# Issuing one kind of input copy from GpSimd's queue instead of SyncE's, in a polynomial convolution with attention

## The chip, the cores and the metric

The kernel runs on one core of a Trainium2 chip. The metric is the device time of one execution in microseconds. The core has a matrix engine (TensorE, PE in the profile), three engines for elementwise work (VectorE or DVE, ScalarE or ACT, GpSimd or POOL), and SyncE (SP), which in this kernel only issues data transfers (DMAs). Each engine works through its own list of instructions in order and waits at an instruction until the semaphores that it names have been raised.

## The reference

Input `x` has 32 images of 64 channels by 56 x 56 pixels. Layer 0 acts on groups of 8 channels; layer 1 is an attention over the 3136 pixels of each image.

```
# layer 0: second and third order products of the 8 channels of a group
p2 = x[:, :, _I2] * x[:, :, _J2]
y2 = einsum('bgihw,goi->bgohw', p2, W2) + b2
p3 = x[:, :, _I3] * x[:, :, _J3] * x[:, :, _K3]
y3 = einsum('bgihw,goi->bgohw', p3, W3) + b3
y  = x + y2 * beta2 + y3 * beta3 * 0.1
# layer 1, l = y
g     = clip(bn(conv1x1(l, w_inside)), 0, 6)
theta = l[:, :32]
f     = einsum('niab,nicd->nabcd', theta, theta)
f     = softmax(softmax(f, over the first pixel index), over the second)
out   = einsum('nabcd,nicd->niab', f, g) / h * w
out   = bn(depthwise_conv3x3(out, w_dw)) + l
```

## The kernel before, in words

The images are worked on in 16 pairs. For each pair a **stage** of 49 tiles runs (24 tiles of 128 pixel rows for the first image, one tile of both images' last 64 rows, 24 for the second image). A tile's scores come from PE into PSUM in two halves, DVE moves them to SBUF and keeps the minimum (the softmax's shift), ACT makes both exponentials over 128 x 3136 elements, and PE multiplies the result with `g` into the accumulators `av` and `ax`. While the tiles of one pair run, the polynomials (layer 0) of the next pair are worked out in between; the convolution taps of the pair before run on DVE, and the rest is `g`, transposes and stores.

Before the first stage the first image's polynomial is computed by itself (to about 90 us). The first stage then has more to do than the others: the second image of the first pair (chunks called two-image chunks here: 32-row halves `TWO = (2, 3)`) and the whole second pair (four-image chunks, `ALL`; the four are the two images' halves of 32 channels). Later stages work out one pair's polynomials each, 13 four-image chunks.

**A chunk.** The 3136 pixels are cut into 13 chunks of 242 (the last 232). The inputs of a chunk are copies of `x` from HBM whose rows are rotated within the groups of channels, so that a product of two tiles multiplies different channels. Per half there are: `x0`, `xa` (the names of their tiles are x and xa in the profile), `x2`, `x4` (both x in the profile), one copy each, and `xb`, two copies of half the rows. Per chunk there is one tile `xc`, filled by two copies: the channels unrotated and rotated by four. These two are the last that a chunk needs. So SP issues 14 copies for a two-image chunk and 26 for a four-image chunk. POOL multiplies: first `q = x0 * xa` per half, then `p = q * x0`, `q * x2`, `q * x4`, `q * xb` per half, and last one product of the two parts of `xc` (called p4 in the code, p<-xc_None in the profile). These go to PE, which accumulates them in six rounds (`poly`, L455); DVE then adds bias and the unrotated part of `xc` and writes `y` (`poly_out`, L472).

**What sets the order.** A class `Pinned` (its `call`, L107; all its instructions have line L108 in the profile) chains every instruction of an engine to the one recorded before it, so that each engine's list is in the order in which the code was run. The copies stand in `plan`, a list in the order of use. `prefetch` (L357) takes the next copies from it while two conditions hold: a buffer is to be had (`XB`, L318: 7 for `x0`, 13 for `xs`, which is all other rotated tiles, 3 for `xc`), and `credit` is at least 1. Each transfer that `start` (L325) issues costs one credit. `pace` (L943) gives 8 (first stage) or 4.5 (later) credits in each half tile, never more than 8 in hand. `prefetch` is called by `advance` (L413) twice per tile and after each product inside `products` (L365), which releases a buffer. Products are limited by `ROOM` (L362): 8 buffers for `q`, 20 for `p`; a chunk of four has 17 p. Loads of `th` (the theta rows, from `y`), the placing of the transposed attention output in `tt`, and the stores to the output go through `start` too, on SP's queue.

Of the kernel before, what the change touches and what calls it, by code (L numbers as in the profile page):

```python
# [69 lines left out]
def tile_poly_conv_attention(  # L70
# [43 lines left out]
    pe, dve, act, pool, sync = map(Pinned, (nc.tensor, nc.vector, nc.scalar, nc.gpsimd, nc.sync))  # L114
# [17 lines left out]
    at = 0  # L132
    for s, (_, bs) in enumerate(STEPS):
        for h in range(2) if s < NSLOT else ():
            act.dma_start(
                out=wq[s::NSLOT, :, h, :],
                in_=wpoly[h * 32 : h * 32 + 32, at : at + NRND, h * 32 : h * 32 + 32],
# [18 lines left out]
    for k in range(2):  # L156
        pe.matmul(
            out=ax[:, k * 256 : k * 256 + 256],
            lhsT=w4,
            rhs=wq.rearrange("p k h o -> p (k h o)")[:, :256],  # L160
            start=(k == 0),
# [105 lines left out]
    for k in range(NRND):  # L267
        by = row("beta2_0") if k == 0 else b3row
        w = wq[:, k, :, :].rearrange("p h o -> p (h o)")
        dve.tensor_tensor(w, w, by, ALU.mult)  # L270
    for half in (0, C):
        w = w4[:, half : half + C]
# [49 lines left out]
    PACE = 4.5  # L322
    credit = [1e9]

    def start(out, in_):  # L325
        credit[0] -= 1
        sync.dma_start(out=out, in_=in_)

    def load_next():
        tag, key = plan.pop(0)  # L330
        n, c, ks, name, k = key
        p0, w = PCS[c]
        held[tag] += 1
        ident = f"{n}_{c}_{ks[0]}_{k}"
        if name == "c":
            t = xp.tile([128, 2, PCH], FP, name=f"xc_{ident}", tag=tag, bufs=XB[tag])
            at = slice(ks[0] * 32, ks[-1] * 32 + 32)
            for d in range(2):
                src = bass.AP(
                    x.tensor,  # L340
                    ((4 * n + ks[0]) * EXT + 4 * d) * 4 * N + p0,
                    [[EXT * 4 * N, len(ks)], [N, 32], [1, w]],
                )
                start(t[at, d, :w], src)
            loaded[key] = [t[at, d, :w] for d in range(2)]
            return
        t = xp.tile([128, PCH], FP, name=f"x{name}_{ident}", tag=tag, bufs=XB[tag])
        for s0, every, d, grow in LOADS[name]:
            src = bass.AP(
                x.tensor,  # L350
                ((4 * n + k) * EXT + d) * 4 * N + p0,
                [[N, 32], [grow * 4 * N, NSLOT // every], [1, w]],
            )
            start(t[s0::every, :w] if every > 1 else t[:, :w], src)
        loaded[key] = t[:, :w]

    def prefetch():  # L357
        while plan and held[plan[0][0]] < XB[plan[0][0]] and credit[0] >= 1:
            load_next()
# [126 lines left out]
    def load_theta(b, c0=0, c1=N):  # L486
        y = ys[b // 2 % 3]
        p0 = (b % 2) * C
        if c0 == 0:
            ths[b] = thp.tile([128, N], FP, name=f"th_{b}", tag=f"th{b % 2}")  # L490
        for r in range(4):
            start(ths[b][r * 32 : r * 32 + 32, c0:c1], y[p0 : p0 + CRED, c0:c1])
# [365 lines left out]
    for n in range(NP):  # L858
# [8 lines left out]
        if n == 0:  # L867
# [10 lines left out]
            at = [2 * base + free[i * (len(free) - 1) // (len(todo) - 1)] for i in range(len(todo))]  # L878
        elif n + 1 == NP:
            todo = gb  # L880
            at = [2 * (base + LAG) + 3 + 4 * i for i in range(len(gb))]
        else:
            at = []
# [30 lines left out]
        for b, end in ((2 * n, base + NQ), (2 * n + 1, base + IT - 1)):  # L914
            t = end + LAG
# [7 lines left out]
    for n in range(NP):  # L923
# [11 lines left out]
        for i in range(9 * NB):  # L935
            at = more[i * (len(more) - 1) // (9 * NB - 1)]
# [11 lines left out]
    t = 0  # L948
# [117 lines left out]
```

## Time and profile before

| | |
|---|---|
| median of 3 runs | 4949.45 us (4947.52 to 4963.6) |
| the profiled execution | 4948.12 us |
| its span | 4946.3 us, mean granted clock 0.992 |
| PE busy | 4734.2 us (96%) |
| ACT busy | 4554.4 us (92%) |
| DVE busy | 4125.5 us (83%) |
| POOL busy | 3222.6 us (65%) |
| SP's transfers of xc | 416, issue 523 to 751 ns, median 561 |
| DMA, mean | 139 GB/s |

Groups in the profile are named by what they write and read: `p<-q,x` is a product of q and an x tile, `ax<-p,wq` a matmul of the polynomial, `ps<-th` the scores, `av<-gq,e` the attention product. SPq is SP's queue with the time that it takes to issue one transfer; issuing is not counted as an engine's busy time. A wait is told as "who <- whom: us in total, times, longest". In an order of time, a line holds the start, the time taken, the engine and the group, how many instructions are merged in it, and in square brackets how long the engine had been idle and what ended that.

### The profile page before, as it was taken

The numbers are of one execution on the slowest core, as the hardware profiler recorded it, in microseconds if no ns is written. First come the engines' busy times: TensorE is split into PE (matmuls) and PEld (weight loads), VectorE is DVE, ScalarE is ACT, GpSimd is POOL, SyncE is SP. The second block draws the span as 40 slices with busy tenths as digits, with TensorE's granted clock in tenths as the row PEclk, the third lists the DMA queues.
The fourth block names the chain that finished last, engine by engine and source line by source line (L and its number), as shares of the span: only waits on it lengthen the run. The fifth ranks groups of instructions, "written<-read, shape, count | busy, mean of one in ns | idle before, by whom it ended". The sixth has DMA issues, their size and how long they took to land.

```text
span 4946.3 us, 264020 instructions
## 1 busy us (share of the span) xinstructions
PE 4734.2 (96%) x118122; PEld 3218.8 (65%) x118122; DVE 4125.5 (83%) x6100; ACT 4554.4 (92%) x2356; POOL 3222.6 (65%) x4335
## 2 busy tenths in 40 slices
PE   6898999999999999999999999999999999999887
PEld 2555666666666666666666666666666666666665
DVE  6545898888888898888889889898888889888887
ACT  1667999999999999999999999999999999999996
POOL 2677685858858586785857768585875858678000
PEclk8999999999999999999999999999999999999999
DMA  7555656565565655556555565656556565654201
GB/s 205 145 152 156 147 144 153 144 152 141 145 141 151 146 145 149 143 143 146 149 143 144 149 143 142 154 144 150 142 145 143 150 144 144 153 142 126 45 11 34
DMA packets 884318, 685.66 MB, mean 139 GB/s; under 512 B 290924, under 2 KB 869356, under 8 KB 879084
## 3 DMA queue, kind: packets, MB, share of 16 engines
q1 hardware_dynamic: 875180, 659.46, 52.5%
q8 instruction: 924, 15.14, 1.3%
q10 hardware_dynamic: 8000, 9.30, 0.6%
q14 instruction: 214, 1.75, 0.1%
HBM read 565.65 MB, written 25.69 MB: 120 GB/s over the span
## 4 chain that ended last, share of the span: by engine, by line
PE 77%; DVE 12%; DMA 3%; issue 3%; ACT 3%; POOL 1%; SPq 1%; ACTq 0%; DVEq 0%; POOLq 0%
PE av L108 33%; PE ps L108 26%; PE ax L108 18%; DVE e L108 10%; ACT e L108 3%; DMA xc_None<-in_x_dram 1%; POOL p L108 1%; DVE y L108 1%; DMA first<-in_x_dram 1%; DVE num L108 1%; DMA x<-in_x_dram 1%; SPq L108 1%; DMA xa<-in_x_dram 0%; DVE rd L108 0%; ACTq L108 0%
## 5 line engine op out<-in xcount | busy, mean ns | idle before, releaser
L108 PEld LDWEIGHTS av<-gq,e 128*64 128x64 f32 x64512 | 2012.2, 138 | 943.9 <-issue 936.2
L108 ACT ACTIVATE e<-e,nm 128x3136 f32<-128x3136 f32 x784 | 2283.6, 2913 | 279.9 <-DVE e L108 264.0
L108 POOL TENSOR_TENSOR p<-q,x 128x242 f32<-128x242 f32 (+1 forms) x2418 | 1824.3, 788 | 815.6 <-PE ax L108 801.2
L108 ACT ACTIVATE e<-e,rz 128x3136 f32<-128x3136 f32 x784 | 2270.3, 2896 | 0.0
L108 PE MATMUL av<-gq,e 128*64 128x65 f32 x64512 | 2225.5, 225 | 3.9 <-ACT e L108 3.1
L108 DVE TENSOR_SCALAR_CACHE_REDUCE e<-ps 128x1568 f32<-128x1568 f32 x784 | 1403.7, 1790 | 314.1 <-PE ps L108 294.2
L108 DVE TENSOR_SCALAR_CACHE_REDUCE e<-ps,nm 128x1568 f32<-128x1568 f32 x784 | 1448.6, 1848 | 255.7 <-PE ps L108 250.1
L108 PE MATMUL ps<-th 32*64 32x392 f32 x25088 | 1449.4, 515 | 120.7 <-DVE e L108 110.7
L108 POOL TENSOR_TENSOR q<-x,xa 128x242 f32<-128x242 f32 x806 | 574.2, 734 | 226.0 <-DMA xa<-in_x_dram 218.0
L108 DVE SCALAR_TENSOR_TENSOR y<-tt,wdt,y 128x605 f32<-128x605 f32 (+6 forms) x711 | 713.1, 1003 | 6.4 <-DMA tt<-tr 5.2
L108 POOL TENSOR_TENSOR p<-q,xb 128x242 f32<-128x242 f32 x806 | 573.9, 739 | 212.3 <-PE ax L108 204.5
L108 PEld LDWEIGHTS ps<-th 32*64 32x64 f32 x25088 | 369.8, 130 | 463.7 <-DVE e L108 381.5
L108 PE MATMUL ax<-gq,e 128*64 128x65 f32 x12288 | 489.7, 222 | 0.7 <-issue 0.6
L108 PE MATMUL ax<-p,wq 128*32 128x242 f32 (+1 forms) x6448 | 481.9, 374 | 1.8 <-POOL p L108 0.2
L108 PEld LDWEIGHTS ax<-gq,e 128*64 128x64 f32 x12288 | 425.0, 138 | 1.0 <-issue 1.0
L108 PEld LDWEIGHTS ax<-p,wq 128*32 128x32 f32 x6448 | 178.4, 109 | 111.8 <-POOL p L108 19.1
L108 POOL TENSOR_SCALAR y<-y,bias 128x616 f32<-128x616 f32 (+2 forms) x79 | 146.9, 1860 | 98.9 <-PE ax L108 98.9
L108 POOL TENSOR_TENSOR p<-xc_None 128x242 f32<-128x242 f32 (+3 forms) x208 | 127.6, 614 | 109.5 <-DMA xc_None<-in_x_dram 91.0
L108 DVE SCALAR_TENSOR_TENSOR y<-ax,bias,xc_None 128x242 f32<-128x242 f32 (+3 forms) x208 | 97.1, 467 | 116.8 <-PE ax L108 116.8
L108 PE MATMUL ax<-wit,y 128*64 128x64 f32 x3136 | 144.2, 223 | 11.7 <-issue 7.5
L108 PE MATMUL ax<-p,w 128*32 128x242 f32 (+1 forms) x1612 | 123.9, 370 | 32.1 <-POOL p L108 32.1
L108 ACT ACTIVATION_READ_ACCUMULATOR e<-e,nm 128x1 f32 x784 | 145.5, 186 | 0.0
(86 smaller groups left out, 1389.4 us busy)
## 6 DMA issues: line engine op xcount, KB each, us to landing
x<-in_x_dram SPq DMA_DIRECT2D x2232, 121.0 KB
xa<-in_x_dram SPq DMA_DIRECT2D x744, 121.0 KB
xb<-in_x_dram SPq DMA_DIRECT2D x1488, 60.5 KB
th<-y SPq DMA_DIRECT2D x124, 392.0 KB
xc_None<-in_x_dram SPq DMA_DIRECT2D x360, 121.0 KB
x<-in_x_dram SPq DMA_DIRECT2D x186, 116.0 KB
out_dram<-y SPq DMA_DIRECT2D x60, 308.0 KB
tt<-tr SPq DMA_DIRECT2D x128, 100.0 KB
```

Of the source, the lines that this page charges most:

```text
L108: i = f(*args, **kw)
```

## The change

`start` gets an argument for the queue, and the two copies that fill `xc` are given POOL's. POOL's queue is in the same order as its products, so the transfers take a place between these. They no longer cost a credit. The rest of the copies stay on SP's queue. The first pair's first image does not use this code.

```diff
-    def start(out, in_):
-        credit[0] -= 1
-        sync.dma_start(out=out, in_=in_)
+    def start(out, in_, queue=sync):
+        if queue is sync:
+            credit[0] -= 1
+        queue.dma_start(out=out, in_=in_)
...
-                start(t[at, d, :w], src)
+                start(t[at, d, :w], src, pool)
```

In the built program POOL's list then has 416 transfers more, and SP's 416 fewer.

## The prediction

> **What bounds the kernel now.** I went from the widest view to the narrowest: busy time by stretch, who waits for whom, then the queues that the change touches, in order of time. Busy time first: the two parts of the first stage (first pair's missing polynomials, 97 to 213 us, then the second pair's, 213 to 482) beside a later stage. Columns are engine busy times, granted clock, DMA share and GB/s.
>
> ```profile
> core 0: us, PE busy (x) PEld busy (x) DVE busy (x) ACT busy (x) POOL busy (x), PEclk, DMA share, GB/s
> 97.00:213.00 116.00, 100.78 (x1876) 57.25 (x1876) 59.33 (x93) 77.67 (x41) 87.25 (x133) 0.98 0.54 143
> 213.00:482.00 269.00, 243.81 (x5360) 153.56 (x5360) 152.11 (x241) 191.83 (x100) 196.18 (x295) 0.96 0.57 151
> 1615.00:1919.00 304.00, 298.27 (x7652) 205.57 (x7646) 266.27 (x388) 294.60 (x154) 215.08 (x288) 1.00 0.57 144
> ```
>
> In a later stage TensorE (PE) and ScalarE (ACT) are full, 298 and 295 of 304 us, and GpSimd (POOL) has 89 us free. In the first stage nothing is full: ACT does 270 us of work in 385. Something feeds it too slowly. The waits of weight loads (PEld) and matmuls between 97 and 482 say what:
>
> ```profile
> PEld ax L108 <- POOL p L108: 62.3, 63, 3.8
> PE ax L108 <- POOL p L108: 32.3, 20, 3.4
> ```
>
> PE waits 95 us for POOL's products; from 1007 to 4650 it waits for POOL not once. And POOL, over that later stretch:
>
> ```profile
> POOL p L108 <- PE ax L108: 890.4, 291, 28.4
> POOL p L108 <- DMA xc_None<-in_x_dram: 20.0, 14, 2.6
> ```
>
> There POOL is ahead: it waits for PE to free product buffers, 890/3643 of the time, or 74 us in each 304. In the first stage it waits for data instead. The order of time of one four-image chunk, on POOL and on SyncE's queue (SPq):
>
> ```profile
> 430.87 7.98 POOL L108 TENSOR_TENSOR p<-q,x 128x242 f32<-128x242 f32 x12
> 438.79 2.70 POOL L108 TENSOR_TENSOR p<-q,xb 128x242 f32<-128x242 f32 x4
> 444.52 0.62 POOL L108 TENSOR_TENSOR p<-xc_None 128x242 f32<-128x242 f32 x1 [3.03 <-DMA xc_None<-in_x_dram]
> ```
> ```profile
> 428.16 5.63 SPq L108 DMA_DIRECT2D x<-in_x_dram  x8
> 433.88 5.05 SPq L108 DMA_DIRECT2D xb<-in_x_dram  x8
> 439.02 1.17 SPq L108 DMA_DIRECT2D xc_None<-in_x_dram  x2
> 440.24 0.56 SPq L108 DMA_DIRECT2D x<-in_x_dram  x1
> ```
>
> SPq issues without a pause, some 0.65 us from one copy to the next, while DMA engines are 57% busy. The pair xc comes last of its chunk, and POOL stands 3.03 us waiting for it. So the first stage is bound by **SPq's issuing**, with POOL just behind; everything later is bound by PE and ACT.
>
> **What the change does, step by step.** The profiled execution took 4948.1 us (span 4946.3); the median of the runs is 4949.45, 1.3 above. My sums start from 4948.1.
>
> *SPq loses* two of 14 copies in a two-image chunk, two of 26 in a four-image one. By the lines above a pair takes 440.24 - 439.02 = 1.2 us. Two-image chunks: their xc products start at 97.50 and, twelve chunks on, at 213.00, so 9.63 us each; SPq would need 8.4. Four-image chunks: from 259.67 to 481.48 is twelve of 18.5 us (the one before, 28.2 us, holds a 9.35 us wait for PE and is left out); SPq would need 17.3. The copies no longer take credit, but SP's queue keeps its order apart from two things: the first image's th copy of each later pair stands behind two more loads (1.3 us), four tt copies behind two. No PE wait for th was seen from 1007 on, so I cost that at nothing; without cover it is 1.3 us in 14 stages, 18 us.
>
> *POOL gains* 416 copies, and its order shows where: a pair stands between products, 12 to 17 products ahead of the one that needs it (0, 2 and 6 for the first three). Twelve products of 0.665 us are 8.0 us; from the issue of the pair above to its product are 444.52 - 439.02 = 5.5 us. So the 55 us in which POOL waits for xc in this stage go, the first wait apart. Most pairs add a wait for DVE, for the chunk three back to have left its xc buffer. Behind it stand POOL's next products, and for those PE; but these wait in any case for PE to free product buffers of a later chunk (20 buffers, 17 to a chunk), so I cost the wait at nothing; uncovered it is at most DVE's 1.85 us operation ahead of it, in the stage's 26 chunks 48 us.
>
> *What one copy costs POOL's queue* no row shows: nothing was issued there. From below: the same copy on SPq, 0.56 us (median of 416). From above: 2.0 us, POOL's longest regular operation (y<-y,bias, 672 columns, 1.99). I take **1.0 us**, nearest to SPq's row, which is the same work, plus some 0.4 for handing it to the engine's cores (POOL's small operations on 128 partitions, a 128-column memset and a 128-column scaling, take 0.2 and 0.64).
>
> The Trainium skill ("DMA: Bandwidth & Descriptors", Latency and other measured facts) gives about 0.6 us to the first byte from SyncE's queue and about 1 us from GpSimd's; as an estimate by that ratio a copy would cost 0.93 us, and the sum would be 2 us lower than mine.
>
> *The sum.* POOL's own pace, waits taken out: two-image chunk 164.24 - 155.73 - 1.16 = 7.35 us; four-image chunk 444.52 - 427.10 - 3.03 - 0.50 = 13.9. With 2.0 us more: 9.35 and 15.9. Each chunk takes the slower of the two queues.
> - Two-image: max(8.4, 9.35) against 9.63, -0.28 x 12 = -3 us. Relief of one queue is eaten by the other.
> - Four-image: max(17.3, 15.9) against 18.5, -1.2 x 13 = -16 us.
> - Later stages: 26 x 1.0 = 26 us more POOL work in each 304, under 74 us of waiting for PE: 0.
>
> Check on the whole: POOL is busy 283 us of the 385; with 52 it is 335 of 366, 92%, full but not over. All of the gain reaches the end, as PE alone could do such a stage in 304. **4948 - 19 = 4929 us.** At the lower bound, 0.56: two-image max(8.4, 8.47), -14, and -16: 4918. At 2.0: +1.72 x 12 = +21, four-image 17.9, -8: 4961.
>
> One page speaks against the move. DVE's only copies here go to PSUM (ax<-bias1r, 288 of 361 ns) and its large reductions come from PSUM; POOL's products in the first stage run at an even 0.665 us beside them. The skill ("SBUF — State Buffer", SBUF: two separate sides, and the section after it) says that a DVE copy in a two-port mode locks GpSimd out of writing descriptors, and that a copy of about 0.62 us then took about 3.1; as an estimate, by 3.1 the same formula would give 4948 + 48 + 21 = 5017, and by 0.62 about 4920. The trace of before can't show it; as the page asks for both ends in SBUF, I do not take it.
>
> **The rivals.**
> 1. *POOL becomes the bound* (slower). Place: the first stage. Mechanism: POOL is held for the whole of each pair, from issue until its data can be used, 5.5 us by the chunk above, so 2.75 a copy. Two-image chunks 12.85, +3.2 x 12 = +39; four-image 19.4, +0.9 x 13 = +12; later 13 x 5.5 = 72 us just under the 74. 4948 + 51 = **4999**. It passes +0.3% from about 2.05 us a copy. For it: POOL is 73 to 75% busy in the first stage, the tightest place for it. Against: its products do not wait for the copy at once.
> 2. *The relief and the load cancel* (no change). At 1.5 us a copy: two-image 10.35, +9; four-image still SPq's 17.3, -16; sum **4941**. Slots freed later by POOL, behind a pair, would make SPq wait in its turn (it already waits 54 us for p between 90 and 450) and take part of the 16.
> 3. *The copies were not what POOL lacked.* Between 90 and 450 POOL also waits 15 for xa, 18 for PE; if these grow by what xc loses, the 55 us come back and POOL's additions show whole: 52 us at most, less SPq's 31: **4969**.
>
> **Chances.** A change under 0.3%, about 15 us, is no more than this measurement can tell from none. By the formula that means faster below about 1.15 us a copy, slower above about 2.05. Forecast (below 1.15): 0.38. Cancelling (1.15 to 2.05, the shift small): 0.32. Rival 1: 0.20; rival 3: 0.10, both slower. As gains and losses share the chance, the likeliest case's own range is 4918 to 4934. The range reaches from just below the lower bound, 4914, to rival 1's 4999.
>
> **What would show it.** In the changed trace: POOLq with 416 xc issues, their duration the disputed size; POOL's wait for xc between 97 and 482 from 55 to under 6 us; xc products 9.4 us apart in the two-image part, 17.3 in the four-image part; the second part's end (481.5, the first xc product of the third pair) near 463; PE still without a wait for POOL from 1007 on, stages still 304 us. The forecast is wrong if issues are over 1.15 us, if SPq's waits for POOL grow by more than it saves, or if a later stage lengthens: a single us there is 14 in all.

## The result, and the profile after

The changed kernel takes 5317.08 us (median of 4 runs, 5299.51 to 5331.99), the kernel before in the same comparison 4949.88 us. The ratio is 1.073, with a 95% interval from 1.071 to 1.076: 7% slower. The forecast of 4929 us and its range, up to 4999 us, are both wrong.

The profiled execution of the changed kernel took 5331.99 us (span 5330.2). Where do the 384 us over the profiled 4948.12 lie? I count a stage from the read-out that ends ScalarE's (ACT's) first exponential of a pair; these moments, counted from the span's start, split the difference:

| | before | after | difference |
|---|---|---|---|
| second stage begins | 505.9 | 489.1 | -17 |
| mean of the 14 stages that follow, to the start of the last | 293.6 | 322.1 | +28.5 each, +399 |
| from there to the end of the trace | 329.7 | 331.4 | +2 |

So the first stage did about what was forecast, and the later stages lost 28.5 us each on the mean (17 to 36). The later stage of 304 us in the prediction was a window a little longer than a stage, which is 293.6 us.

**The first stage.** Four-image chunk, order of time (start, time taken, engine, group, count, idle before):

```profile
408.92 6.16 SPq L108 DMA_DIRECT2D x<-in_x_dram  x8
...
411.61 1.37 POOL L108 DMA_DIRECT2D xc_None<-in_x_dram  x2
...
412.99 7.94 POOL L108 TENSOR_TENSOR p<-q,x 128x242 f32<-128x242 f32 x12
...
415.18 5.04 SPq L108 DMA_DIRECT2D xb<-in_x_dram  x8
...
420.27 0.59 SPq L108 DMA_DIRECT2D x<-in_x_dram  x1
...
420.90 2.68 POOL L108 TENSOR_TENSOR p<-q,xb 128x242 f32<-128x242 f32 x4
...
423.55 0.61 POOL L108 TENSOR_TENSOR p<-xc_None 128x242 f32<-128x242 f32 x1
```

The pair stands between GpSimd's (POOL's) products, 1.37 us for two copies. SyncE's queue (SPq) goes from xb to the next chunk's x with no xc between them, and the product of xc starts without an idle time in brackets: 3.03 us of waiting are gone.

**The later stages.** The same windows as before (the first two cut at 203 and 459 us, near the new ends of the two parts, 206.4 and 458.5); the third is the later stretch from 1615 to 1919:

```profile
core 0: us, PE busy (x) PEld busy (x) DVE busy (x) ACT busy (x) POOL busy (x), PEclk, DMA share, GB/s
97.00:203.00 106.00, 101.89 (x1806) 55.75 (x1808) 57.30 (x89) 72.65 (x38) 99.84 (x151) 0.97 0.63 160
203.00:459.00 256.00, 243.96 (x5418) 151.60 (x5420) 153.74 (x246) 196.46 (x102) 217.43 (x329) 0.99 0.62 156
1615.00:1919.00 304.00, 280.96 (x7016) 193.06 (x7024) 258.83 (x359) 272.51 (x141) 207.11 (x285) 0.97 0.54 132
```

In the third row ACT is down from 294.60 to 272.51 us and TensorE (PE) from 298.27 to 280.96. Neither is full any more, POOL is not full either, and less data is moved (144 to 132 GB/s). So something makes all of them wait. The waits of the whole run (who waits for whom: us in total, times, longest), first before, then after:

```profile
POOL p L108 <- PE ax L108: 1018.8, 331, 28.4
...
PEld ps L108 <- DVE e L108: 381.5, 886, 3.2
ACT e L108 <- DVE e L108: 264.0, 359, 23.9
...
PE ps L108 <- DVE e L108: 110.7, 256, 2.0
...
POOL p L108 <- DMA xc_None<-in_x_dram: 91.0, 44, 4.9
```
```profile
POOL p L108 <- PE ax L108: 1339.5, 302, 34.4
...
PEld ps L108 <- DVE e L108: 655.6, 896, 9.0
ACT e L108 <- DVE e L108: 651.7, 461, 23.9
PE ps L108 <- DVE e L108: 388.7, 334, 8.5
...
POOL p L108 <- DMA xc_None<-in_x_dram: 7.4, 2, 4.8
```

ACT's wait for VectorE's (DVE's) minimum and move `e` went from 264.0 to 651.7 us, PE's from 110.7 to 388.7. POOL still waits for PE, by 1339.5 us where it was 1018.8: POOL is not the bound, and everything is late behind DVE. What in DVE became longer is told by its groups by shape, before (xcount, busy us, mean ns of one, idle before):

```profile
L108 DVE TENSOR_SCALAR_CACHE_REDUCE e<-ps 128x1568 f32<-128x1568 f32 x784 | 1403.7, 1790 | 314.1 <-PE ps L108 294.2
L108 DVE SCALAR_TENSOR_TENSOR y<-tt,wdt,y 128x605 f32<-128x605 f32 x360 | 370.7, 1030 | 0.0
L108 DVE SCALAR_TENSOR_TENSOR y<-tt,wdt,y 128x616 f32<-128x616 f32 x180 | 167.0, 928 | 0.0
```

and after:

```profile
L108 DVE TENSOR_SCALAR_CACHE_REDUCE e<-ps 128x1568 f32<-128x1568 f32 x784 | 1403.3, 1790 | 362.9 <-PE ps L108 347.4
L108 DVE SCALAR_TENSOR_TENSOR y<-tt,wdt,y 128x605 f32<-128x605 f32 x360 | 556.0, 1544 | 0.0
L108 DVE SCALAR_TENSOR_TENSOR y<-tt,wdt,y 128x616 f32<-128x616 f32 x180 | 249.1, 1384 | 0.0
```

The large reductions take what they took; the convolution **taps** `y<-tt,wdt,y` take half as long again. A mean hides how: of all 711 taps the longest took 1.5 us before; after, 89 took over 2.5 us (I call these held taps), the longest 9.8 us, and the sum went from 713 to 1011 us. One of them in order of time:

```profile
1883.94 2.71 POOL L108 TENSOR_TENSOR q<-x,xa 128x242 f32<-128x242 f32 x4
...
1886.57 1.37 POOL L108 DMA_DIRECT2D xc_None<-in_x_dram  x2
...
1887.95 5.24 POOL L108 TENSOR_TENSOR p<-q,x 128x242 f32<-128x242 f32 x7
...
1888.66 3.97 DVE L108 SCALAR_TENSOR_TENSOR y<-tt,wdt,y 128x616 f32<-128x616 f32 x1
...
1892.55 1.84 DVE L108 TENSOR_SCALAR_CACHE_REDUCE e<-ps,nm 128x1568 f32<-128x1568 f32 x1
...
1894.44 2.91 ACT L108 ACTIVATE e<-e,nm 128x3136 f32<-128x3136 f32 x1 [2.73 <-DVE e L108]
...
1894.46 1.24 PE L108 MATMUL ps<-th 32*64 32x392 f32 x16 [2.60 <-DVE e L108]
```

POOL issues a pair, then runs seven products without a pause. The tap that begins 0.7 us behind the pair takes 3.97 us instead of about 0.9, and ends within the seventh product, which takes 1.23 us where the others take 0.7: only ahead of that one did it get in. The reduction queued behind it on DVE is late, and ACT and PE stand idle for 2.73 and 2.60 us. In all, 73 of the 96 taps that began within 2.5 us behind a pair, without a pause of POOL over 0.15 us between, were held; of other DVE work that began within 1.3 us behind a pair, none grew (49 large reductions and 28 transposes among it).

Not every held tap begins near a pair, but going back from each of the 89 over POOL's list without a pause leads to one. In 14 of them, one in each later stage, POOL's own `y<-y,bias` stands between, and the tap begins some 5 us after its end, 9.7 us behind the pair. Behind a `y<-y,bias` that a pause parts from the pair no tap was held.

PE loses once more: its matmuls are the same and its busy time went from 4734.2 to 4834.5 us, with the mean granted clock from 0.992 to 0.970. The clock alone would give 4734.2 x 0.992 / 0.970 = 4842, so it is enough to account for the growth. Before, PE was never idle for longer than 0.84 us between 1007 and 4650, at a clock of 1.00; after, 66 of its gaps there are over 2 us, at 0.97.

### The profile page after: what moved, and what is told of

It reads as the page before. It is cut to its first block, busy times and chain, and to the rows that moved or that the text cites. A ratio compares the mean times of both kernels' runs of the same rounds, so it can differ in the third digit from the quotient of the medians.

```text
span 5330.2 us, 263929 instructions
## 1 busy us (share of the span) xinstructions
PE 4834.5 (91%) x118122; PEld 3269.8 (61%) x118122; DVE 4416.9 (83%) x6100; ACT 4554.3 (85%) x2356; POOL 3442.3 (65%) x4751
## 4 chain that ended last, share of the span: by engine, by line
PE 64%; DVE 17%; issue 10%; DMA 3%; POOL 2%; ACT 2%; SPq 1%; ACTq 0%; POOLq 0%; DVEq 0%
PE av L108 27%; PE ps L108 22%; DVE e L108 14%; PE ax L108 14%; ACT e L108 2%; POOL p L108 2%; DVE y L108 2%; DMA x<-in_x_dram 1%; SPq L108 1%; DVE num L108 1%; DMA xa<-in_x_dram 1%; DMA first<-in_x_dram 1%; DMA xb<-in_x_dram 0%; PE first_s L108 0%; POOL xc_None L108 0%
## 5 line engine op out<-in xcount | busy, mean ns | idle before, releaser
L108 ACT ACTIVATE e<-e,nm 128x3136 f32<-128x3136 f32 x784 | 2283.5, 2913 | 662.0 <-DVE e L108 651.7
L108 PEld LDWEIGHTS av<-gq,e 128*64 128x64 f32 x64512 | 2051.4, 140 | 981.6 <-issue 975.1
L108 POOL TENSOR_TENSOR p<-q,x 128x242 f32<-128x242 f32 (+1 forms) x2418 | 1769.0, 765 | 1017.1 <-PE ax L108 990.5
L108 PE MATMUL av<-gq,e 128*64 128x65 f32 x64512 | 2267.8, 227 | 19.0 <-issue 15.9
L108 PE MATMUL ps<-th 32*64 32x392 f32 x25088 | 1475.3, 523 | 407.9 <-DVE e L108 388.7
L108 DVE SCALAR_TENSOR_TENSOR y<-tt,wdt,y 128x605 f32<-128x605 f32 (+6 forms) x711 | 1011.0, 1422 | 6.4 <-DMA tt<-tr 5.2
L108 POOL TENSOR_TENSOR q<-x,xa 128x242 f32<-128x242 f32 x806 | 560.5, 723 | 149.6 <-DMA xa<-in_x_dram 144.9
L108 PE MATMUL ax<-p,wq 128*32 128x242 f32 (+1 forms) x6448 | 509.7, 386 | 7.7 <-POOL p L108 5.9
L108 POOL DMA_DIRECT2D xc_None<-in_x_dram x416 | 288.0, 693 | 0.8 <-issue 0.7
L108 PE MATMUL ax<-q,wq 128*32 128x242 f32 x1612 | 130.4, 380 | 3.3 <-POOL q L108 3.1
```

What stands on the lines that cost most here:

```text
L108: i = f(*args, **kw)
```

## The experiments

The theory was: issuing copies on POOL leaves it in a state in which its products follow each other without letting DVE's taps in, and a held tap makes ACT and PE late. The rivals: the copies' bytes and landing hold DVE; or the order of the loads, changed by the credit, does it. The table holds the runs' results (e1, e2 and e12 are medians of 4 to 10 executions, the other experiments single ones); kernel before on the same chips: 4945.9 to 4947.3 us. "Near" are taps that began within 2.5 us behind the interposed operations, with no pause of POOL over 0.15 us between.

| run | us | later stage, us | taps, sum us | held taps, longest us | held of near |
|---|---|---|---|---|---|
| before | 4946 | 293.6 | 713 | 0, 1.5 | - |
| after | 5317 | 322.1 | 1011 | 89, 9.8 | 73 of 96 |
| e1_credit_only | 4947.5 | 293.6 | 713 | 0, 1.5 | - |
| e2_first_stage_only | 4926.0 | 293.7 | 717 | 0, 1.5 | - |
| e3_no_taps_sp | 4946.5 | 293.4 | 24 | 0, 0.7 | - |
| e4_no_taps_pool | 4940.8 | 294.3 | 24 | 0, 0.7 | - |
| e5_resync | 4975.7 | 296.7 | 771 | 13, 3.2 | 0 of 86 |
| e6_before_pause | 5102.0 | 306.3 | 841 | 31, 10.9 | 30 of 35 |
| e7_tiny_copies | 5234.5 | 314.0 | 948 | 60, 9.2 | 41 of 93 |
| e8_one_row | 5244.2 | 314.6 | 975 | 58, 9.5 | 43 of 103 |
| e9_memset_alone | 5314.8 | 321.0 | 1004 | 88, 9.8 | 71 of 92 |
| e10_memset_for_pair | 5005.0 | 297.7 | 771 | 15, 4.0 | 13 of 96 |
| e11_one_input_taps | 5190.8 | 312.4 | 750 | 92, 5.9 | 65 of 98 |
| e12_act_first_stage | 4959.7 | 293.5 | 713 | 0, 1.5 | - |
| e13_scaling_for_pair | 5049.1 | 300.7 | 775 | 21, 7.4 | 20 of 93 |
| e14_single_copy | 5228.8 | 315.2 | 928 | 74, 8.8 | 52 of 90 |
| e15_one_input_taps_sp | 4945.5 | 293.4 | 485 | 0, 1.1 | - |

### Order, place or taps

**e1_credit_only** (before, without credit for xc):

```diff
-    def start(out, in_):
-        credit[0] -= 1
+    def start(out, in_, cost=1):
+        credit[0] -= cost
...
-                start(t[at, d, :w], src)
+                start(t[at, d, :w], src, 0)
```

> The kernel before with one edit: the two unrotated copies stay on SyncE's queue, but cost no credit, so that the loads behind them are begun as early as in the changed kernel. My theory (GpSimd's issuing holds up VectorE's convolution taps, which read two SBUF tiles): nothing of the loss is here, 4949 us within 15, a later stage 294 us, no tap over 1.5 us. The rival that the order and credit of the loads did it: near 5317 us, a later stage near 322, taps up to 9 us.

Measured: 4947.54 us, ratio 1.0003 (0.9993 to 1.0013). The credit and the order of the loads have no part in the loss.

**e2_first_stage_only** (after, POOL's queue for the first two pairs only):

```diff
-                start(t[at, d, :w], src, pool)
+                start(t[at, d, :w], src, pool if n < 2 else sync)
```

> The changed kernel, with GpSimd's queue used only for the copies that are begun for the first two pairs (all of them needed in the first stage, in which no taps run); from the third pair on the copies are SyncE's again. My theory: the first stage keeps its gain of 17 us (first exponential of the second stage near 389 us) and the later stages are 294 us again, so 4931 us, faster than both kernels, no tap over 1.5 us. A rival by which something set up in the first stage (the earlier loads, the order) slows what follows: over 4960 us, stages over 294. If the gain of the first stage were only work pushed into the second: near 4949.

Measured: 4925.97 us (4925.22 to 4927.91), ratio 0.996 (0.9945 to 0.9975). (The 389 us in the expectation is the length of the first stage by another count; by the starts used above the second stage begins at 479.8 us.) A later window of this kernel, and its taps:

```profile
1600.00:1904.00 304.00, 298.71 (x7663) 206.06 (x7656) 265.61 (x388) 294.81 (x153) 218.32 (x292) 1.00 0.56 147
```
```profile
L108 DVE SCALAR_TENSOR_TENSOR y<-tt,wdt,y 128x605 f32<-128x605 f32 x360 | 370.7, 1030 | 0.0
```

PE and ACT are full again and the taps are those of before. The gain of the first stage stays and reaches the end. This kernel beats both others, by 20 us and by some 390 us. It begins its second stage 9 us earlier than the changed kernel; I did not follow these 9 us.

**e3_no_taps_sp** and **e4_no_taps_pool** (before and after, with these lines at the start of `conv_step`):

```diff
+        if n + 1 < NP:
+            return
```

> The kernel before with VectorE's convolution taps left out for the first 15 pairs (that part of the computation is missing); it is the base for the run that follows. All theories: 4949 us or less, since a later stage loses some 51 us of VectorE's work and its matmuls remain: 4750 to 4950 us, stages 280 to 294.

> The changed kernel with the same taps left out. My theory (the taps are what is held): about 17 us less than the run without taps on SyncE's queue, later stages equal in both within 1 us, no VectorE operation lengthened. The rival that transfers or the loads' order slow the later stages, whatever VectorE does: 300 to 400 us more than the run without taps on SyncE's queue. The rival that GpSimd's issuing slows every two-input or SBUF operation: something between, 50 to 300 us more.

Measured: 4946.46 and 4940.77 us. With the taps goes the whole loss: POOL's 416 copies then cost the later stages 0.8 us each, not 28.5. The second run is 5.7 us shorter than the first, where I expected about 17. That the first run isn't shorter than the kernel before shows that the taps fill DVE's spare time and cost nothing while they aren't held. The 0.8 us are not spread evenly: five stages took 294.3 to 299.0 us, the other nine 293.4 to 293.7. In the 14 stages PE stood idle for 10.9 us (1.7 in the first run) before instructions for which the trace shows no wait; what made it idle stays open. Loads of theta rows are not it, though their waits grew in the run with POOL's copies:

```profile
PEld ps L108 <- DMA th<-y: 11.8, 6, 4.3
...
PE ps L108 <- DMA th<-y: 10.2, 5, 4.3
```
```profile
475.01 0.29 PEld L108 LDWEIGHTS ps<-th 32*64 32x64 f32 x4 [4.29 <-DMA th<-y]
475.01 1.57 PE L108 MATMUL ps<-th 32*64 32x392 f32 x4 [3.01 <-DMA th<-y]
```

The totals were 6.5 and 3.2 us with SyncE's. But all of these waits lie ahead of the second stage, and a weight load (PEld) and a matmul often wait in the same stretch, as in the two lines. Counted once, the waits just ahead of the second stage are 13.6 us, 5.9 with SyncE's; in the 14 stages that follow there is none in either run.

### What in the pair does it

**e5_resync** (after, with two operations behind each pair):

```diff
+    mark = const.tile([128, 2], FP, name="mark")
...
+            pool.memset(mark[:, :1], 0.0)
+            pool.tensor_scalar(mark[:, 1:], mark[:, :1], 1.0, None, ALU.add)
```

> The changed kernel with two small operations on GpSimd behind each pair: a memset of one column and a scaling that reads it (so that it has to wait for the memset), which brings GpSimd's cores together again. My theory (the products behind a pair run on cores that are out of step, so that reads of SBUF overlap without a gap in which a tap could get in): taps over 3 us gone, later stages 294 to 298 us, 4930 to 4990 us. The rivals (the copies' transfers, or any GpSimd issue beside a tap): as the changed kernel, 5317 us, and some us more.

Measured: 4975.74 us, within the range of the theory, though 13 taps over 3 us were left. In order of time:

```profile
2475.15 1.41 POOL L108 DMA_DIRECT2D xc_None<-in_x_dram  x2
...
2476.55 0.12 POOL L108 MEMSET mark<- 128x1 f32 x1
...
2476.76 0.21 POOL L108 TENSOR_SCALAR mark<-mark 128x1 f32<-128x1 f32 x1
...
2476.94 4.50 POOL L108 TENSOR_TENSOR p<-q,x 128x242 f32<-128x242 f32 x5
...
2476.97 0.08 DVE L108 DVE_READ_ACCUMULATOR e<-ps 128x1 f32 x1
2476.97 1.31 DVE L108 SCALAR_TENSOR_TENSOR y<-tt,wdt,y 128x605 f32<-128x605 f32 x1
```

The same pair, the same products without a pause, and a tap that begins 0.4 us behind the pair takes 1.31 us. No near tap was held. The 13 that were held begin some 4.8 us behind the end of POOL's y<-y,bias, one in each of 13 stages, and take 3.2 us, as the 14 of the changed kernel do at that place. A pair and its two operations stand 2.7 us ahead of that y<-y,bias, four products and no pause between; so the two operations do not free every tap of the row behind them.

**e6_before_pause** (after; pairs issued at another place of POOL's list):

```diff
+    later = []
...
-                start(t[at, d, :w], src, pool)
+                if n < 2:
+                    start(t[at, d, :w], src, pool)
+                else:
+                    later.append((t[at, d, :w], src))
...
+                if (of, k) == ("2", 3):
+                    while later:
+                        start(*later.pop(0), pool)
```

> The changed kernel, in which the pairs from the third on are issued at another place of GpSimd's list: just before the product at which it waits for TensorE to free a buffer in most chunks of the later stages. The same number of copies, bytes and issues on the same queue. My theory: GpSimd pauses soon after the pair, so that a held tap ends with the pause; taps over 3 us nearly gone, stages 294 to 302, 4930 to 5050 us. The rival that the transfers or the issuing as such lengthen the taps: near 5317 us.

Measured: 5102.01 us, beyond my range, but far from 5317. The reason for the miss is that POOL does not wait at that place in every chunk. Where it did wait between pair and tap, none of 116 taps was held; where it did not, 30 of 35 were. Within the same 2.5 us behind the pair, the pause makes the difference.

**e7_tiny_copies** and **e8_one_row** (before; xc on SyncE, and POOL issues copies that nobody reads, of 128 rows by one element, or of one row):

```diff
+    spare = const.tile([128, 2], FP, name="spare")
...
+                if n > 1:
+                    pool.dma_start(out=spare[:, d : d + 1], in_=bass.AP(x.tensor, p0, [[N, 128], [1, 1]]))
```
```diff
+                    pool.dma_start(out=spare[:1, d : d + 1], in_=bass.AP(x.tensor, p0, [[N, 1], [1, 1]]))
```

> The kernel before, with its unrotated copies on SyncE's queue; GpSimd issues, at the place where the changed kernel has its pairs (from the third pair of images on), two copies of 128 rows by one element into a spare tile that nobody reads. As many descriptors as the real ones, 1/242 of the bytes. My theory (issuing does it): the later stages lengthen as in the changed kernel, near 320 us, with taps up to 9 us; 5250 to 5350 us. The rival that the bytes or their landing do it: 4949 us within 15.

> As the run with small copies, but each copy is one row of one element, one descriptor in place of 128. My theory, if what matters is how long the generation of descriptors keeps some of GpSimd's cores: far fewer held taps, 4949 to 5100 us. If any issue, however short, is enough: near 5317 us. The rival that the bytes do it: 4949 us within 15.

Measured: 5234.52 and 5244.18 us, the first a little below what I expected. The rival of the bytes is out: 1/242 of them, or next to none, leave most of the loss. What I had expected of one row, far fewer held taps since there is little to generate, is wrong as well: 58 against 60. (By the profile's DMA packets the two runs are alike, 32 for each copy, where a real copy has 128. So they may not differ in what there is to generate, and they don't settle whether that matters.) The issues' own time hardly differs either, by the groups of the run with one row (mean of the small copies 558 ns, of one row 546, of the real ones 693):

```profile
L108 POOL DMA_DIRECT2D spare<-in_x_dram x364 | 197.1, 546 | 0.0
```

**e9_memset_alone** (the run e5 without the scaling, so that nothing waits):

```diff
+            pool.memset(mark[:, :1], 0.0)
```

> As the run with two small operations behind each pair (4976 us), but with the memset of one column alone: nothing on GpSimd waits for it. If what helped was the wait, in which GpSimd's cores come together: as the changed kernel, 5250 to 5330 us, taps up to 9 us. If what helped was that any other operation stood between the pair and the products: 4950 to 5000 us, no tap over 4 us behind a pair.

Measured: 5314.81 us, like the changed kernel.

```profile
L108 DVE SCALAR_TENSOR_TENSOR y<-tt,wdt,y 128x605 f32<-128x605 f32 x360 | 557.7, 1549 | 0.0
```

A memset behind the pair does nothing; the cure was the scaling that waits for it. That it was the wait, and not the scaling as such, is likely but not shown: a scaling behind a pair that waits for nothing was not run. In e13 scalings without a wait did not free the taps behind them.

**e10_memset_for_pair** and **e13_scaling_for_pair** (before; other POOL operations in place of the issue):

```diff
+    spare = const.tile([128, 256], FP, name="spare")
...
+                if n > 1:
+                    for j in range(4 * d, 4 * d + 4):
+                        pool.memset(spare[:, 32 * j : 32 * j + 32], 0.0)
```
```diff
+    spare = const.tile([128, 256], FP, name="spare")
+    pool.memset(spare, 0.0)
...
+                if n > 1:
+                    half = spare[:, 128 * d : 128 * d + 128]
+                    pool.tensor_scalar(half, half, 1.0, None, ALU.mult)
```

> The kernel before, copies on SyncE's queue; at the place of each pair from the third pair of images on, GpSimd makes eight memsets of 32 columns, about as long as a pair's issue (1 to 1.4 us). If only the issue of a copy starts the holding of taps: 4949 us within 15, no tap over 1.5 us. The rival that any break of some 1 us in GpSimd's row of products does it: 5200 to 5330 us, taps up to 9 us.

> The kernel before, copies on SyncE's queue; at the place of each pair from the third pair of images on, GpSimd scales two spare blocks of 128 columns in place (0.64 us each by the profile before, 1.3 us together, as long as a pair's issue), and nothing waits for them. If the issue of a copy is what starts the holding: 4949 to 5010 us, at most the 13 taps of the run with memsets. If any break of that length in the row of products does it: as the changed kernel, 5250 to 5330 us, with 60 or more taps over 3 us.

Measured: 5005.03 and 5049.06 us, between the two sides in both runs. The memsets took 0.54 us in all, less than the 1 to 1.4 I had aimed at, the scalings 1.03. Neither view holds whole: a break in the products without any copy does hold taps (13 of 96, 20 of 93), but far fewer than a copy.

**e14_single_copy** (after; only the first copy of a pair on POOL):

```diff
-                start(t[at, d, :w], src, pool)
+                start(t[at, d, :w], src, sync if d and n > 1 else pool)
```

> The changed kernel, but from the third pair of images on the second copy of each pair is SyncE's again, so that GpSimd issues one copy per chunk instead of two, 0.69 us for 1.37. If any issue is enough: near 5317 us. If the length of the break decides, by the runs so far (13 held taps at 0.54 us, 43 at 1.07, over 70 at 1.37): 15 to 35 held taps, 5000 to 5150 us.

Measured: 5228.81 us, 74 held taps, between the two sides and nearer to the first. The length of the break does not decide: one copy of 0.70 us held 52 of 90 near taps, two scalings of 1.03 us held 20 of 93. What stands in the break does: the issue of a copy holds more taps than a longer break without one. A second copy adds to it (73 of 96).

### Which operation is held

**e11_one_input_taps** (after) and **e15_one_input_taps_sp** (the same, all copies on SyncE), each tap now

```diff
-        dve.scalar_tensor_tensor(
+        dve.tensor_scalar(
             yr,
             tr[:, r0 + dy - 1 : r1 + dy - 1, x0 + dx - 1 : x1 + dx - 1],
             wdt[:, k : k + 1],
-            yr,
+            None,
             ALU.mult,
-            ALU.add,
         )
```

> The changed kernel; each tap is a scaling that reads one SBUF tile (the attention output) and overwrites the output block, instead of a scaling and an addition that read two (the sum over the nine taps is left out). My theory (a tap is held because it reads two SBUF inputs, as the products do): no tap held, later stages 293 to 296 us, 4925 to 4965 us. The rival that any VectorE operation from SBUF to SBUF is held at such a place: over 5100 us, taps over 3 us.

> The taps as scalings that read one SBUF tile (the sum over the nine taps is left out), with all copies on SyncE's queue: the base of the run that had them with GpSimd's copies (5191 us). If these taps are held by GpSimd's issuing alone: 4935 to 4955 us, no tap over 1.5 us. If such taps meet GpSimd's products badly in any case: over 5000 us.

Measured: 5190.81 and 4945.50 us. First with POOL's copies, then with SyncE's:

```profile
L108 DVE TENSOR_SCALAR y<-tt,wdt 128x605 f32<-128x605 f32 x360 | 393.0, 1092 | 0.0
```
```profile
L108 DVE TENSOR_SCALAR y<-tt,wdt 128x605 f32<-128x605 f32 x360 | 260.0, 722 | 0.0
```

My theory had it that a tap is held because it reads two SBUF tiles. That part is wrong: a scaling that reads one is held too, 65 of 98 near ones. The transposes, which also go from SBUF to SBUF, are not (at most 1012 ns in the changed kernel). So some kinds of DVE operation are held and others not, and two inputs is not the whole mark.

The Trainium skill ("SBUF — State Buffer", SBUF: two separate sides) says that DVE and GpSimd share one pair of SBUF ports under an exclusive lock, held for a whole instruction, and that DVE needs it with two SBUF inputs against a GpSimd operation that reads SBUF, or in a two-port mode. That two-input taps are held and reductions from PSUM are not agrees with it. The scalings fit it too: the shortest in e15 take 0.45 us for 448 columns and 0.55 for 672, 0.46 ns for a further column, where the taps of the kernel before take 0.68 and 0.89, 0.96 ns. Half the time for a column would fit a two-port mode; the mode itself no run shows. By that rule a tap should wait for one product, 0.7 us, as it does in the kernel before (605 columns: 0.82 us at the shortest, 1.42 at the longest). That in the changed kernel 4 to 14 products come to their end while one held tap lasts, up to 9.8 us, the page does not say, and here the measurement stands alone.

### Another queue for the first stage

**e12_act_first_stage** (the copies of the first two pairs from ACT's queue):

```diff
-                start(t[at, d, :w], src, pool)
+                start(t[at, d, :w], src, act if n < 2 else sync)
```

> The copies of the first two pairs of images are issued from ScalarE's queue instead of GpSimd's, all later ones from SyncE's. If the gain of the first stage is the relief of SyncE alone, it is kept or grows, since GpSimd issues nothing: two-image chunks 8.4 us for 9.63, four-image chunks 17.3 for 18.5, in all 4948 - 31 = 4917 us; ScalarE has 115 of 385 us free there. If the copies come late, because they stand behind activations that wait for VectorE: 4930 to 4960 us, and GpSimd waits for xc again.

Measured: 4959.73 us, ratio 1.0031 (1.0021 to 1.0041). The second stage begins at 515.2 us, 9 later than before; later stages are 293.5.

```profile
ACT e L108 <- POOL p L108: 54.5, 11, 7.8
POOL p L108 <- DMA xc_None<-in_x_dram: 48.8, 24, 6.8
...
ACT e L108 <- DMA x<-in_x_dram: 28.2, 3, 11.2
```

ACT, which never waited for POOL's products or for x before, now does: a copy that waits for its buffer holds the exponentials behind it. Relief of SyncE is not enough; the queue that takes the copies must have its turn for them at the right time, as POOL's, between the products that use them, has.

## Why the prediction was wrong, point by point

- **What bounds the first stage: right.** SPq's issuing bound it. Two-image chunks came 8.97 us apart on the mean, 8.79 once steady (the formula with the measured copy gives 8.73; before 9.63), four-image chunks 17.4 (forecast 17.3). The first xc product of the third pair started at 458.5 us (forecast 463), and POOL's wait for xc in all fell from 91.0 to 7.4 us.
- **The price of a copy on POOL's queue: 0.69 us** (661 to 900 ns in the profile), between the bounds, 0.3 below the value taken. With 0.69 the formula gives a gain of some 27 us; up to the first xc product of the third pair 23 were won, and at the beginning of the second stage 17 were left. That this is near the forecast 19 is partly luck: the price was taken too high, and something was lost that the sum did not hold (next but one).
- **The rivals that were about POOL's time: not met.** POOL was not held until the data landed, and PE waited less for it than before. None of the rivals named the later stages' loss, though the prediction's last sentence named a longer later stage as a sign against it.
- **The order of theta rows, costed at nothing in 14 stages: right there,** since PE does not wait for theta rows in a later stage of any run. Just ahead of the second stage, where the term did not look, these waits went from 6.4 to 12.2 us (PE and its weight loads counted once), which is most of the difference between the 23 us and the 17. Since the same order without POOL's queue (e1) left them at 6.3, the order alone is not their cause, and that stays open.
- **"Later stages: 26 x 1.0 = 26 us more POOL work in each 304, under 74 us of waiting for PE: 0": this step failed.** As time of POOL it was right: POOL has room. The term measured 28.5 us a stage, 399 in all, because POOL's list does something to another engine, which a sum of busy times by engine does not hold: 89 of DVE's 711 taps were held for 3 to 9.8 us, and ACT and PE waited behind them. The taps are a DVE row that I did not look at.
- **The page that spoke against the move was turned down for too narrow a reason.** I asked whether DVE's copies could lock out POOL's descriptors and looked for copies from SBUF to SBUF. The harm went the other way, from POOL to DVE, and hit the taps, which read SBUF beside POOL's products. The 3.1 us per copy of that page, and the 5017 us from it, are not what happened either: a copy's issue stayed at 0.69 us. (The 5017 was also added up too low: at 3.1 us, 26 copies are 81 us a later stage, over the 74 that the same sum allows.)

In every run, POOL's list leads back from each held tap to a copy's issue, or to what stands in its place, without a pause of POOL over 0.15 us.

What is shown: the issue of copies on POOL, whatever their bytes, in a later stage, leads to taps that last from 2.5 to 10.9 us (the longest in e6) until POOL pauses or the row of products lets them in; without the taps the loss is gone, and with two operations behind the pair, of which one waits for the other, it is nearly so. What stays open is the state inside POOL. That its cores are out of step behind an issue, and come together at a wait, fits e5 and e9, but nothing here shows the cores; that POOL's list of begun instructions runs further ahead behind a break, and stops doing so at a wait, fits e5, e9, e10 and e13, and does not tell why one copy is worse than a longer scaling. Nor is it told why a held tap most often gets in ahead of the seventh product of its row (61 of the 89 in the changed kernel), and at times only ahead of the fifteenth (8).

## What to carry to other kernels

Before work is put on an idle engine, look at what else shares something with it: list the operations of the other engines that run beside the new instructions, and ask which could be held, even where the idle engine has room for all of the time. Here a copy on GpSimd's queue was cheap in the stage in which no taps ran on VectorE beside GpSimd's products, and dear where they did: restrict it to the stage that needs it (here 20 us won instead of 367 lost). If it must stand elsewhere, try an operation of GpSimd behind it that waits for another (4976 us in e5, still 29 above the kernel before). And look at the longest instruction of each group, not at means alone.

## What the runs showed of the hardware that was not expected

- A copy of 128 rows takes POOL 0.69 us to issue, one of one row by one element 0.55; SyncE takes 0.56 for the former. In the changed kernel the landing took 4.7 us from issue for xc on POOL's queue, 3.0 for x on SyncE's; the trace of before has no landings, so xc on SyncE's queue can't be set beside it.
- With copies issued on POOL, a tap lasted up to 9.8 us in the changed kernel, while 14 products came to their end; in the kernel before no tap was over 1.5 us. Scalings in the place of copies (e13) led to 7.4 us at most, and to fewer held taps.
- A memset and a scaling of 0.2 us that waits for it, put behind the pair on POOL, made near taps free again (0 of 86 held); the memset alone did nothing (71 of 92).
- PE's idle time came with a lower clock: the same matmuls took 100 us longer at a mean granted clock of 0.970 instead of 0.992. In e13, e6 and e7, 5049, 5102 and 5235 us long, it was 0.984, 0.982 and 0.974.
